# A hybrid transformer block in one core: the keys of 13 feed-forward blocks as seven products over both token halves, linear attention in buffers of its own, and a new order of the work

## The chip, the core and the metric

The kernel runs on one core of a Trainium2 chip. A core has five engines, each with an instruction queue that it works through in order: TensorE (PE, matmuls; its weight loads are listed apart as PEld), VectorE (DVE), ScalarE (ACT), GpSimd (POOL) and SyncE (SP, which here only issues DMAs). They wait for each other through semaphores. The metric is the device time of one execution in microseconds; the time before is 1154.61 us, the median of three runs (1153.1 to 1155.28).

## The reference

x has the shape (8, 512, 256): 8 batches of 512 tokens with 256 features, in float32. Four residual steps follow, each with a layer norm in front (LN):

```python
x = x + attn_a(LN(x))      # linear attention: l2norm(x Wq) * mean over tokens of l2norm(x Wk) * (x Wv)
x = x + ffn(LN(x))         # the first ffn, "f"
x = x + attn_b(LN(x))      # softmax attention, 16 heads of 64; the softmax runs over the queries
x = x + ffn(LN(x))         # the second ffn, "g", with the same weights
```

The ffn mixes each token with the one before it, with one weight per feature, and gates:

```python
xr = mu_r * x + (1 - mu_r) * x_prev
xk = mu_k * x + (1 - mu_k) * x_prev
out = sigmoid(xr @ Wr.T) * (square(relu(xk @ Wk.T)) @ Wv.T)
```

## The kernel before, in words

A batch is held as four tiles of 128 tokens, and most steps run on one half of a batch (256 tokens, h = 0 or 1). Features are put on the partitions by transposing, so a half is two chunks of 128 features by 256 tokens. All matmuls are in float32.

**Softmax attention** is the frame of the program. The 16 heads of a batch are 8 pairs; g counts pairs over all batches (64). For a pair, `scores` (L1007) makes four chunks of scores with small 64x64 matmuls (L1019), VectorE takes their maximum (nm, L1024), `exps` (L1029) makes the exponents e and their sums on ScalarE (L1035), `scale_v` (L1043) has VectorE invert the sums (rs, L1048) and GpSimd scale the values (vs, L1052), and `context` (L1059) multiplies e with vs (cx, L1072). `attend` (L1085) runs two pairs, with the scores of one beside the context of the other. The e tiles come from a pool of six buffers.

**Projections.** For batches after the first, queries, keys and values come from seven products in place of eight, in Strassen's manner: `seven` (L794) takes the two halves of the tokens and the two halves of the features as a 2x2 block matrix. Its weights' sums are made once (`sums_of_weights`, L745), the rows' sums once a batch with four GpSimd subtractions (`sums_of_rows`, L759, L775). Each chain of seven uses three PSUM banks; VectorE and ScalarE add the products up between the matmuls (L814, L824, L832, L866, L874), and three products (numbers 2, 3 and 4) are accumulated onto a bank that was read before.

**The ffn** (`ffn`, L523) runs half by half: mixing, the keys (L533, four matmuls of 128x256 for each half), relu and square on ScalarE (L540, L543), the gate r, the output o, and two element-wise steps (L552, L559). For batches 0 and 1, and for the last ffn g7, features get onto the partitions by PE transposes (`mixed_t`, L449). The other 13 ffns, f2 to f7 and g0 to g6, do it by DMA (`mixed_dma`, L487): GpSimd sets the 16-bit halves apart (L411), SP issues a DMA transpose (L416), GpSimd puts them together again (L420).

**Linear attention** (`linear`, L592; `queries`, L642; `mean`, L662; `front`, L678) shares the tiles xn, xp, xr and xk of the f ffns. There are two such sets: one for batch 1 and for g0 to g6 (True in tile names), one for all else (False). `add_front` (L570) begins linear attention of batch b when the whole first ffn of the batch ahead is done.

**The order** of all this is fixed when the program is built. Class `Order` (L77) is a planner: each piece of work is a generator that yields steps with an engine, an assumed duration and a time from which it can run; the planner keeps a clock for each engine and decides which step is issued next. Pieces have due times counted in pairs (`due_of`, L578). After each two pairs of heads, `until` (L212) issues what is due, and `fill` (L197) more, up to a share of the remaining PE work. `CHOICES` (L38) has a triple for each two pairs: an offset to that share, a slack for the other engines, and a number that shuffles the ranks. Each PSUM bank that a piece holds is tracked (`take`, `give`, `clear`).

**Loads and stores.** When both halves of g of batch b are done, SP stores them (L976) and loads x of batch b + 4, 512 KB (`load_x`, L266, its DMA on L271). SP's queue has these loads and stores and all DMA transposes. At the end, after the last context, the output projection y of batch 7 is followed by g7, with what is left of g6 between.

Of the kernel before, what the change touches and what calls it, by code (L numbers as in the profile page):

```python
# [9 lines left out]
U16 = mybir.dt.uint16  # L10
# [28 lines left out]
    (-4, 2, 90203), (-4, -1, 82533), (-6, 1, 13258), (1, 2, 55349), (6, -1, 0), (6, 0, 31648),  # L39
    (6, 1, 79266), (-6, 2, 0), (6, 2, 0), (-6, 0, 0), (6, 2, 32685), (0, 0, 0), (6, -1, 57850),  # L40
    (2, 2, 0), (-2, 0, 61030), (0, 0, 8722), (0, -1, 70803), (6, -1, 0), (1, 0, 423),
    (0, 0, 1350), (-1, 0, 93496), (-6, -1, 32755), (6, 1, 0), (1, 2, 25961), (4, 0, 78747),
    (1, 2, 30264), (0, 2, 52830), (4, 2, 36824), (6, 0, 37004), (4, -1, 19765), (-2, 1, 75445),
    (0, 0, 79050), (6, 1, 84670), (4, 1, 42587),
# [32 lines left out]
class Order:  # L77
# [40 lines left out]
    def clear(self, banks):  # L118

        for i in banks:  # L120
            while not unheld(self.banks[i]):
                c = self.banks[i]
                self.run(c if c.mark in self.marks else self.first(self.able()))
# [111 lines left out]
def kernel(ctx: ExitStack, tc: tile.TileContext, a: dict, out: bass.AP):  # L235
# [20 lines left out]
    epool = ctx.enter_context(tc.tile_pool(name="epool", bufs=6))  # L256
# [71 lines left out]
    def buffers(own):  # L328


        if own not in sets:
            s = {
                n: one.tile([P, 2, 512], F32, tag=f"{n}{own}", name=f"{n}{own}")
                for n in ("xr", "xk")
            }
            for n in ("xn", "xp"):
                s[n] = one.tile([P, 2, 2, HS + 1], F32, tag=f"{n}{own}", name=f"{n}{own}")
                nc.gpsimd.memset(s[n][:, 0, :, 0:1], 0.0)

            s["ka"], s["r"] = s["xn"], s["xk"]  # L340
            sets[own] = s
        return sets[own]

# [3 lines left out]

    def inner(t, h):
        return t[:, h, :, 1:]
# [5 lines left out]
    def normed(src, name, s, h, ready, early=False):  # L355
# [7 lines left out]
        xn, rstd = inner(s["xn"], h), small.tile([P, 2], F32, tag="rstd", name=f"rstd_{name}_{h}")  # L363
# [27 lines left out]
    def normed_t(src, name, s, h, ready, mark=None, early=False):  # L391

        ready = yield from normed(src, name, s, h, ready, early)
        xn = inner(s["xn"], h)
        ready = yield "T", 0.55, ready, -1, mark
        ps = bank(f"tr_{name}_{h}").rearrange("p (k s) -> p k s", k=KC)
        for kc in range(KC):
            for u in range(2):
                nc.tensor.transpose(
                    ps[:, kc, u * P : (u + 1) * P], xn[:, u, kc * P : (kc + 1) * P], ident  # L400
                )
        return ps, ready

    def normed_dma(src, name, s, h, ready, dst, mark=None):


        ready = yield from normed(src, name, s, h, ready)
        apart, turned = (s[n].bitcast(U16)[:, h, :] for n in ("xr", "xk"))
        ready = yield "G", 1.2, ready
        for u in range(2):  # L410
            nc.gpsimd.tensor_copy(  # L411
                apart.rearrange("p (l k u d) -> p l k u d", l=2, k=KC, u=2)[:, :, :, u, :],
                s["xn"].bitcast(U16)[:, h, u, 2:].rearrange("p (k d l) -> p l k d", l=2, k=KC),
            )
        ready = yield "S", 0.9, ready
        nc.sync.dma_start_transpose(  # L416
            out=turned.rearrange("p (g r) -> p g r", r=P), in_=apart
        )
        ready = yield "G", 1.25, ready, -1, mark
        nc.gpsimd.tensor_copy(  # L420
            dst().rearrange("p k (s l) -> p l k s", l=2),
            turned.rearrange("p (l k s) -> p l k s", l=2, k=KC),
        )
        return ready
# [23 lines left out]

    def mixed_t(xb, name, s, h, ready, xr, xk):  # L449
# [3 lines left out]

        parts = ((1, s["xn"]), (0, s["xp"]))
# [8 lines left out]
        for i, y in parts:  # L463
            for kc in range(KC):
                nc.scalar.activation(
                    y[:, h, kc, 1:], ps[:, kc, :], AF.Identity, scale=omu[:, i, kc : kc + 1]
                )
        order.marks[name, h] = ready
        if h == 1:
            ready = yield "V", 0.25, ready, -1, (name, 0)  # L470
            for i, y in parts:
                nc.vector.tensor_tensor(
                    y[:, 1, :, 0:1], edge[name], omu[:, i, :].unsqueeze(2), ALU.mult
                )
        for (i, y), dst in zip(parts, (xk, xr)):
            ready = yield "V", 0.79, ready
            for kc in range(KC):
                nc.vector.scalar_tensor_tensor(
                    dst[:, kc, :], ps[:, kc, :], mu[:, i, kc : kc + 1], y[:, h, kc, :HS],
# [7 lines left out]
    def mixed_dma(xb, name, s, h, ready, xr, xk):  # L487
# [4 lines left out]
            lambda: s["xr"].bitcast(U16)[:, h, :].rearrange("p (k s) -> p k s", k=KC),  # L492
# [6 lines left out]
        for i, dst in ((1, xk), (0, xr)):  # L499
# [7 lines left out]
            if h == 0:  # L507
                nc.vector.memset(ps[:, :, 0:1], 0.0)
            else:
                nc.vector.tensor_tensor(  # L510
                    ps[:, :, 0:1], edge[name], omu[:, i, :].unsqueeze(2), ALU.mult
                )
# [10 lines left out]
    def ffn(xb, name, s, h, ready, add_on, by_dma):  # L523
# [5 lines left out]
        done = yield "T", BANK, mixed  # L529
        ps = bank(f"k_{name}_{h}")  # L530
        for dc in range(KC):
            for kc in range(KC):
                nc.tensor.matmul(  # L533
                    ps[:, dc * HS : (dc + 1) * HS], lhsT=fk[:, kc, dc * P : (dc + 1) * P],
                    rhs=xk[:, kc, :], start=(kc == 0), stop=(kc == KC - 1),
                )
        done = yield "A", 0.6, done
        ka, r = inner(s["ka"], h), s["r"][:, h, :]
        ps = ps.rearrange("p (k s) -> p k s", k=KC)
        nc.scalar.activation(ka, ps, AF.Relu)  # L540
        order.give()
        squared = yield "A", 0.6, done
        nc.scalar.activation(ka, ka, AF.Square)  # L543
# [5 lines left out]
        ready = yield "T", BANK, squared  # L549
# [4 lines left out]
        return (yield from add_to(xb, h, r, ready, add_on))  # L554

# [14 lines left out]
    def add_front(b):  # L570


        if b in x and b not in begun and (b < 2 or (0 if b == 2 else b - 1) in fronts):
            begun.add(b)
            for h in range(2):
                order.add(linear(b, h), *due_of(b))
# [15 lines left out]
    def linear(b, h):  # L592

        xb, s = x[b], buffers(b == 1)
        ready = asked[b] + X_LANDS[min(b, 2)] + h / 2
        xt, kv = inner(s["xp"], h), inner(s["ka"], h)
# [5 lines left out]
        else:  # L602
            ready = yield from normed_dma(
                xb, f"a{b}", s, h, ready, lambda: s["xp"].bitcast(U16)[:, h, :, 2:]
# [4 lines left out]
        for u in range(2):  # L609
# [10 lines left out]
            sq = one.tile([P, D], F32, tag="sq", name=f"sqk_{b}_{h}_{u}")  # L620
            nc.scalar.activation(sq, ps[:, :D], AF.Square, accum_out=ss[:, u : u + 1])
# [20 lines left out]
    def queries(b, h):  # L642

        s = buffers(b == 1)
        xt = inner(s["xp"], h)
# [4 lines left out]
        for u in range(2):  # L650
            sq = one.tile([P, D], F32, tag="sq", name=f"sqq_{b}_{h}_{u}")
            nc.scalar.activation(
                sq, ps[:, u * D : (u + 1) * D], AF.Square, accum_out=ss[:, u : u + 1]
# [24 lines left out]
    def front(b, h, gf, ready):  # L678
# [4 lines left out]
        rn, qs = halves[b, h], tiles(s["r"], h)  # L683
# [4 lines left out]
        ready = yield from add_to(xb, h, s["r"][:, h, :], ready, adder(b))  # L688
        ready = yield from ffn(xb, f"f{b}", s, h, ready, adder(b), b >= 2)
# [23 lines left out]
        else:  # L713
            if b:
                order.add(sums_of_rows(b, ready), NP * b - 1, NP)
            fronts.add(b)
            if b:
                add_front(b + 1)
# [13 lines left out]
    }  # L732

# [11 lines left out]
    def sums_of_weights(w, tag, split, after):  # L745
# [3 lines left out]
        (a11, a21), (a12, a22) = v  # L749
        s1, s2, s4 = (s[:, i, :].rearrange("p (g c) -> p g c", g=a11.shape[1]) for i in range(3))  # L750
        for dst, x0, x1, op in (
            (s1, a21, a22, ALU.add), (s2, s1, a11, ALU.subtract), (s4, a12, s2, ALU.subtract),
            (a21, a11, a21, ALU.subtract),
        ):
            ready = yield "G", 1.3, 0.0, -1, after
# [29 lines left out]
    def blocks_of_weights(w, sums, split, g):  # L785
# [5 lines left out]
        s1, s2, s4 = (sums[:, i, g * n : (g + 1) * n] for i in range(3))  # L791
        return [a11, a12, s4, a22, s1, s2, s3]

    def seven(name, sums, mul, c, begin, join):  # L794
# [5 lines left out]
        (c11, c12), (c21, c22) = c  # L800

        def product(n):
            ready = yield "T", FAST, 0.0, -1, sums
# [4 lines left out]
            return i, ps, ps.rearrange("p (u s) -> p u s", u=2), ready  # L808
# [4 lines left out]
        u2 = yield "V", 0.62, max(ready, u1)  # L813
# [4 lines left out]
        p2 = yield "T", FAST, u1, -1, None, False  # L818
        mul(b1, 2, False)
        yield from begin(ps1, c11, max(p2, u2))  # L820
        order.give(i1)
        i5, b5, ps5, p5 = yield from product(5)
        c22_done = yield "V", 0.62, max(p5, u3)
        nc.vector.tensor_tensor(c22, ps5, c22, ALU.add)  # L824
        p4 = yield "T", FAST, u3, -1, None, False
        mul(b7, 4, False)
        yield from join(ps7, c21, c12, p4, False)
        order.give(i7)
        p3 = yield "T", FAST, c22_done, -1, None, False
        mul(b5, 3, False)  # L830
        order.marks[name] = yield "V", 0.62, p3
        nc.vector.tensor_tensor(c12, ps5, c12, ALU.add)  # L832
        order.give(i5)

# [110 lines left out]
    def project_out(b, half):  # L945
# [3 lines left out]
        for tp in range(NT // 2):  # L949
# [10 lines left out]
            if half == 1:  # L960
                order.add(tail(b, tp, ready), NP * (b + 2) + 1, lead)
# [3 lines left out]
    def tail(b, h, ready):  # L965
# [7 lines left out]
        order.marks["g", b, h] = yield from ffn(x[b], f"g{b}", buffers(not last), h, ready, add_on, not last)  # L973
# [156 lines left out]
    order.add(sums_of_weights(av, "sums_v", split_values, "plain_v"), 5)  # L1130
    order.until(-1)
# [5 lines left out]
    total += 2 * FAST  # L1137
# [76 lines left out]
```

## Time and profile before

| | us |
|---|---|
| median of three runs | 1154.61 |
| the profiled execution | 1151.33 |
| its span, first to last instruction | 1149.6 |
| PE busy | 1127.1 |
| VectorE (DVE) busy | 780.2 |
| ScalarE (ACT) busy | 671.8 |
| GpSimd (POOL) busy | 440.3 |

The clock granted to TensorE is full throughout. How to read the lines: a group of instructions has the source line, the engine, the operation, the tiles (out<-in), the shape and the count, then its busy time in us and the mean of one in ns, then the idle time of the engine just before these instructions, and what ended it. A line of the timeline has the start and the duration in us, and in brackets the idle time of the engine before it. PE matmuls overlap in the pipeline, so a mean of 379 ns stands for less time on the path. Names are those of the program; xkFalse is the tile xk of the set False.

### The profile page before, as it was taken

What the parts mean: (1) busy time and instruction counts of PE and PEld (TensorE: products, weight loads), DVE (VectorE), ACT (ScalarE), POOL (GpSimd) and SP (SyncE); (2) the same over time, 40 slices, a digit from 0 to 9 for tenths busy, and PEclk for the clock granted to TensorE, in tenths of its full rate; (3) what the DMA queues carried; (4) which work ended last, traced back from release to release, by engine and by line L of the source; (5) the groups of instructions that cost most, each with busy time, mean ns of one, the idle gap of its engine ahead of it and who ended that gap; (6) DMA issues with size and microseconds to landing.
All of it is one profiled execution on the core that took longest, in us unless ns stands there. A gap on an engine that the chain in (4) does not pass through costs nothing.

```text
span 1149.6 us, 19062 instructions
## 1 busy us (share of the span) xinstructions
PE 1127.1 (98%) x7020; PEld 702.6 (61%) x7020; DVE 780.2 (68%) x1403; ACT 671.8 (58%) x1763; POOL 440.3 (38%) x708
## 2 busy tenths in 40 slices
PE   7999999999999999999999899999999999999998
PEld 4645565856556676666667466567665666566557
DVE  5767658676667775867667576667676676666663
ACT  3547646475565654666544675565665367644753
POOL 4455224334324464335612436243453534312201
PEclk9999999999999999999999999999999999999999
DMA  8000001100101101011100201001010011000001
GB/s 297 1 1 2 1 1 19 20 10 11 28 1 42 24 19 28 1 46 29 37 1 1 54 12 38 11 17 40 10 29 19 19 19 25 5 10 19 11 1 37
DMA packets 61180, 28.63 MB, mean 25 GB/s; under 512 B 51456, under 2 KB 59648, under 8 KB 60576
## 3 DMA queue, kind: packets, MB, share of 16 engines
q1 hardware_dynamic: 59936, 25.70, 9.0%
q8 instruction: 56, 0.92, 0.3%
q10 hardware_dynamic: 864, 1.05, 0.3%
q0 software_dynamic: 288, 0.67, 0.2%
q14 instruction: 36, 0.29, 0.1%
HBM read 10.63 MB, written 4.19 MB: 13 GB/s over the span
## 4 chain that ended last, share of the span: by engine, by line
PE 75%; DVE 1%; DMA 0%; issue 0%; ACT 0%; POOL 0%; POOLq 0%; DVEq 0%
PE cx L1072 16%; PE sc L1019 15%; PE m_qk L858 13%; PE y L432 8%; PE m_v L894 6%; PE kv L613 3%; PE o_g L432 2%; PE r_g L432 2%; PE k_g L533 2%; PE k_f L533 2%; PE r_f L432 2%; PE o_f L432 2%; PE q L432 2%; DVE nm L1024 1%; DMA xkFalse<-xrFalse 0%
## 5 line engine op out<-in xcount | busy, mean ns | idle before, releaser
L1035 ACT ACTIVATE e<-sc,nm 128x512 f32<-128x512 f32 x512 | 347.1, 690 | 119.8 <-DVE nm L1024 119.8
L1024 DVE TENSOR_REDUCE nm<-sc 128x2 f32<-128x1024 f32 x256 | 308.9, 1218 | 76.6 <-PE sc L1019 75.7
L1072 PE MATMUL cx<-e,vs 64*64 64x512 f32 x2048 | 265.2, 590 | 5.1 <-POOL vs L1052 4.0
L1019 PE MATMUL sc<-qk 64*64 64x512 f32 x2048 | 266.8, 593 | 1.0 <-DVE qk L832 0.9
L1052 POOL TENSOR_TENSOR vs<-v,rs 128x256 f32<-128x256 f32 x128 | 78.5, 614 | 356.7 <-DVE rs L1048 348.6
L1072 PEld LDWEIGHTS cx<-e,vs 64*64 64x64 f32 x2048 | 84.3, 133 | 143.3 <-issue 117.8
L1019 PEld LDWEIGHTS sc<-qk 64*64 64x64 f32 x2048 | 75.0, 132 | 136.8 <-issue 90.7
L432 PE MATMUL y<-al,ctx 128*128 128x256 f32 x512 | 116.2, 380 | 0.0
L432 PEld LDWEIGHTS y<-al,ctx 128*128 128x128 f32 x512 | 97.0, 190 | 15.8 <-ACT e L1035 1.6
L1035 ACT ACTIVATION_READ_ACCUMULATOR e<-sc,nm 128x1 f32 x512 | 105.2, 205 | 0.0
L866 ACT ACTIVATE qk<-m_qk,bias 128x256 f32<-128x256 f32 x124 | 52.2, 476 | 56.9 <-PE m_qk L858 53.5
L1080 DVE TENSOR_TENSOR ctx<-cx,ctx 128x512 f32<-128x512 f32 x64 | 44.3, 692 | 47.6 <-ACT ctx L1079 47.6
L874 DVE SCALAR_TENSOR_TENSOR qk<-m_qk,dbias,qk 128x256 f32<-128x256 f32 x124 | 54.0, 477 | 18.3 <-PE m_qk L858 17.3
L958 DVE TENSOR_TENSOR x<-y,x 128x512 f32<-128x512 f32 x32 | 22.1, 690 | 55.3 <-PE y L432 55.3
L613 PE MATMUL kv<-wkv,xpFalse 128*128 128x512 f32 x112 | 52.2, 599 | 0.0
L1079 ACT COPY ctx<-cx 128x512 f32<-128x512 f32 x64 | 37.4, 585 | 13.8 <-PE cx L1072 13.8
L619 ACT COPY av<-kv 128x256 f32<-128x256 f32 x32 | 11.9, 373 | 54.8 <-PE kv L613 52.2
L411 POOL COPY xrFalse<-xnFalse 128x512 uint16<-128x512 uint16 x68 | 39.6, 616 | 8.5 <-ACT xnFalse L385 8.5
L559 POOL TENSOR_TENSOR x<-x,xkFalse 128x512 f32<-128x512 f32 x24 | 31.2, 1303 | 27.2 <-issue 8.7
L858 PE MATMUL m_qk<-xta,aq 128*128 128x256 f32 x124 | 39.1, 397 | 0.0
L858 PE MATMUL m_qk<-xta,sums_q 128*128 128x256 f32 x124 | 38.1, 389 | 0.7 <-DVE qk L814 0.7
L858 PE MATMUL m_qk<-xts,aq 128*128 128x256 f32 x124 | 37.2, 382 | 0.3 <-DVE qk L874 0.3
(243 smaller groups left out, 1881.6 us busy)
## 6 DMA issues: line engine op xcount, KB each, us to landing
out<-x SPq DMA_DIRECT2D x16, 256.0 KB, 2.1
x<-in_x SPq DMA_DIRECT2D x6, 512.0 KB, 4.3
aq<-in_aq SPq DMA_DIRECT2D x1, 1024.0 KB, 6.2
ak<-in_ak SPq DMA_DIRECT2D x1, 1024.0 KB, 8.1
av<-in_av SPq DMA_DIRECT2D x1, 1024.0 KB, 10.2
al<-in_al SPq DMA_DIRECT2D x1, 1024.0 KB, 12.2
xkFalse<-xrFalse SPq DMA_TRANSPOSE x34, 3.1
x<-in_x ACTq DMA_DIRECT2D x4, 128.0 KB, 4.0
```

Of the source, the lines that this page charges most:

```text
L432: nc.tensor.matmul(ps[:, u * D : (u + 1) * D], lhsT=lhs[i][:, u * P : (u + 1) * P], rhs=rhs[i], start=(i == 0), stop=(i == n - 1),)
L533: nc.tensor.matmul(ps[:, dc * HS : (dc + 1) * HS], lhsT=fk[:, kc, dc * P : (dc + 1) * P], rhs=xk[:, kc, :], start=(kc == 0), stop=(kc == K ...
L613: nc.tensor.matmul(ps, lhsT=xt[:, kc, u * P : (u + 1) * P], rhs=wkv[:, kc, :], start=(kc == 0), stop=(kc == KC - 1),)
L858: nc.tensor.matmul(ps[:, w * HS : (w + 1) * HS], lhsT=lhs[w][n - 1], rhs=block_of_rows(b, n), start=start and w == 0, stop=True, skip_grou ...
L866: nc.scalar.activation(dst[:, w, :], ps[:, w, :], AF.Identity, bias=bias[:, w, p : p + 1])
L874: nc.vector.scalar_tensor_tensor(dst[:, w, :], ps[:, w, :], dbias[:, w, p // 2 : p // 2 + 1], part[:, w, :], ALU.add, ALU.add,)
L894: nc.tensor.matmul(ps[:, u * HS : (u + 1) * HS], lhsT=block_of_rows(b, n)[:, u * P : (u + 1) * P], rhs=rhs[n - 1], start=start and u == 0, ...
L1019: nc.tensor.matmul(ps[m * HD : (m + 1) * HD, j, :], lhsT=kt[hs, keys], rhs=qt[hs, :], start=True, stop=True,)
L1024: nc.vector.tensor_reduce(nm, ps, AX.X, ALU.max, negate=True)
L1035: nc.scalar.activation(e[:, j, :], ps[:, j, :], AF.Exp, bias=nm[:, j : j + 1], accum_out=sums[g, h][:, c % 2, j : j + 1],)
L1052: nc.gpsimd.tensor_tensor(vs, vh[b, p // 4][:, 2 * h : 2 * h + 2, cols].rearrange("p t (j d) -> p t j d", j=2), rs.unsqueeze(3).to_broadca ...
L1072: nc.tensor.matmul(cx[m][j * HD : (j + 1) * HD, :], lhsT=vsc[g, c // 2][ks, c % 2, j, :], rhs=es[g, c][ks, j, :], start=(c == 0), stop=(c ...
```

## The change

1. **Keys in seven products.** For the 13 ffns with DMA transposes the keys of both halves are made together, when both are mixed, by a new function `keys`. It makes four GpSimd subtractions of 128x256, runs `seven` at half size (one matmul of 128x256 for each product, one PSUM bank each), and then relu and square of each half from SBUF. The sums of the weights fk are made once (four subtractions of 128x128).
2. **Linear attention in its own buffers** for batches from 2 on (`buffers_linear`); it begins when linear attention of the batch ahead is done, and so runs beside that batch's first ffn. An ffn of batch b waits for the one of batch b - 1.
3. **Buffers.** xp goes, xn has no extra column any more, `mixed_t` and the mixing write the previous token's part straight into the target tile; squares whose values nobody needs go to tiles that are free at the time. There are five e buffers in place of six.
4. **Order.** `clear` prefers steps that take no bank; PE's planned total is lower by 13 half products; `CHOICES` has new numbers.

```diff
-    (-4, 2, 90203), (-4, -1, 82533), (-6, 1, 13258), (1, 2, 55349), (6, -1, 0), (6, 0, 31648),
...
+    (-4, 2, 90203), (0, 0, 43155), (0, 2, 0), (-2, 2, 77416), (1, 0, 8249), (-2, 1, 93964),
...
-    epool = ctx.enter_context(tc.tile_pool(name="epool", bufs=6))
+    epool = ctx.enter_context(tc.tile_pool(name="epool", bufs=5))
...
+    def buffers_linear(b):
+        if b < 2:
+            return buffers(b == 1)
+        if "linear" not in sets:
+            n = {n: one.tile([P, 2, 512], F32, tag=f"{n}l", name=f"{n}l") for n in ("xn", "xr")}
+            sets["linear"] = {"xn": n["xn"], "xk": n["xn"], "ka": n["xn"], "xr": n["xr"], "r": n["xr"]}
+        return sets["linear"]
...
+        if by_dma:
+            r, mark = s["xr"][:, h, :], (name, "k", h)
+            if both((name, "k")):
+                order.add(keys(name, s, mixed), *due)
+        else:
...
+    def keys(name, s, ready):
+        xk = [chunks(s["xk"], h) for h in range(2)]
+        (b11, b12), (b21, b22) = ([xk[h][:, kc, :] for h in range(2)] for kc in range(KC))
+        t = s["sums"]
...
+        for dst, x0, x1 in (
+            (t[:, 1, :], b22, b12), (b12, b12, b11), (t[:, 0, :], b22, b12),
+            (t[:, 2, :], b21, t[:, 0, :]),
+        ):
+            ready = yield "G", 0.8, ready
+            nc.gpsimd.tensor_tensor(dst, x0, x1, ALU.subtract)
...
+        def mul(ps, n, start):
+            nc.tensor.matmul(
+                ps[:, :HS], lhsT=lhs[n - 1], rhs=rhs[n - 1], start=start, stop=True,
+                skip_group_check=True,
+            )
+        def begin(ps, dst, ready):
+            ready = yield "A", 0.36, ready
+            nc.scalar.copy(dst, ps)
+            return ready
+        def join(ps, dst, part, ready, first):
+            ready = yield "V", 0.36, ready
+            nc.vector.tensor_tensor(dst, ps, part, ALU.add)
+            return ready
+        def through(h, ready):
+            for f in (AF.Relu, AF.Square):
+                ready = yield "A", 0.6, ready
+                nc.scalar.activation(ka[h], ka[h], f)
+            order.marks[name, "k", h] = ready
+        c = [[ka[h][:, dc, :] for h in range(2)] for dc in range(KC)]
+        yield from seven(f"k_{name}", (name, "t"), mul, c, begin, join, 0.5, through)
...
-        if b in x and b not in begun and (b < 2 or (0 if b == 2 else b - 1) in fronts):
+        if b in x and b not in begun and (b < 3 or b - 1 in fronts):
...
-        ready = yield from add_to(xb, h, s["r"][:, h, :], ready, adder(b))
-        ready = yield from ffn(xb, f"f{b}", s, h, ready, adder(b), b >= 2)
+        ready = yield from add_to(xb, h, q[:, h, :], ready, adder(b))
+        if b > 1:
+            if both(f"l{b}"):
+                fronts.add(b)
+                add_front(b + 1)
+            ready = yield "V", 0.0, ready, -1, (f"n{0 if b == 2 else b - 1}", h)
+        ready = yield from ffn(xb, f"f{b}", s, h, ready, adder(b), b >= 2, due_of(b))
...
-    total += 2 * FAST
+    total += 2 * FAST - 13 * FAST / 2
```

## The prediction

> **What bounds the kernel now.** I read the page first: engine shares, then the costliest groups.
>
> ```profile
> PE 1127.1 (98%) x7020; PEld 702.6 (61%) x7020; DVE 780.2 (68%) x1403; ACT 671.8 (58%) x1763; POOL 440.3 (38%) x708
> L1072 PE MATMUL cx<-e,vs 64*64 64x512 f32 x2048 | 265.2, 590 | 5.1 <-POOL vs L1052 4.0
> L858 PE MATMUL m_qk<-xta,aq 128*128 128x256 f32 x124 | 39.1, 397 | 0.0
> L858 PE MATMUL m_qk<-xta,sums_q 128*128 128x256 f32 x124 | 38.1, 389 | 0.7 <-DVE qk L814 0.7
> L858 PE MATMUL m_qk<-xts,aq 128*128 128x256 f32 x124 | 37.2, 382 | 0.3 <-DVE qk L874 0.3
> L858 PE MATMUL m_qk<-xta,ak 128*128 128x256 f32 x124 | 36.9, 379 | 0.0
> ```
>
> TensorE (PE) is busy for 98% of the span, the next engine (VectorE) for 68%. A busy PE is not a PE at its peak, so I looked at the chain that ended last for a stretch with nothing to wait for:
>
> ```profile
> 269.10 3.45 PE y L432 x16
> ```
>
> An fp32 matmul leaves two records, so 16 records are 8 matmuls of 128x256: 3.45 / 8 = 0.431 us each. At that rate (0.86 us for 512 columns and for a group of four 64x64 ones) the PE work adds up to about 1100 us of the 1149.6 us span. The rest, near 49 us, is 6.9 us before the first matmul, 4.6 after the last, about 10 in the first 100 us, and small losses at each change of work. So time comes from fewer PE cycles, or from the few long PE waits. Two of these are the 4.0 us that cx (L1072) waits for POOL. The timeline around the longer one:
>
> ```profile
> 639.27 0.38 SPq L271 DMA_DIRECT2D x<-in_x  x1
> 639.75 1.25 SPq L416 DMA_TRANSPOSE xkFalse<-xrFalse  x1
> 644.62 1.33 POOL L420 COPY xrFalse<-xkFalse 128x1024 uint16<-128x1024 uint16 x1 [5.38 <-DMA xkFalse<-xrFalse]
> 645.88 1.19 POOL L1052 TENSOR_TENSOR vs<-v,rs 128x256 f32<-128x256 f32 x2
> 646.55 1.09 PE L1072 MATMUL cx<-e,vs 64*64 64x512 f32 x8 [3.39 <-POOL vs L1052]
> ```
>
> A transpose is issued half a microsecond behind the 512 KB load of the next x. It lands after 4.8 us, where the median is 3.1. POOL runs in order, so the copy out of the transpose holds the scaled values (vs), and PE waits 3.39 us. The same happens at 773 us (load 773.23, transpose 773.77, cx idle 0.65): together the 4.0 us of the row.
>
> **The change, part by part.** Sums are made against the profiled execution, 1151.33 us (its span and 1.7 us around it); the median of the runs is 3.28 us above it, and I carry that over.
>
> (a) Seven products. 13 ffns make the keys with 8 matmuls of 128x256 for both halves now (L533), and with 7 afterwards. The built program has 3531 matmuls against 3544 before: -13. Gain 13 x 0.431 = 5.6 us, all on the path.
>
> (b) What the seven products need. Nearest rows, same sizes:
>
> ```profile
> L775 POOL TENSOR_TENSOR xts<-xta 128x256 f32<-128x256 f32 x16 | 11.7, 733 | 1.5 <-PE m_qk L858 1.0
> L625 DVE TENSOR_TENSOR xnFalse<-kv,av 128x256 f32<-128x256 f32 x28 | 11.8, 421 | 25.6 <-ACT sqk L621 25.6
> L619 ACT COPY av<-kv 128x256 f32<-128x256 f32 x32 | 11.9, 373 | 54.8 <-PE kv L613 52.2 <-DVE xnTrue L625 2.0
> ```
>
> Per ffn: four subtractions on POOL, 4 x 0.733 = 2.9 us; five adds on DVE, 5 x 0.421 = 2.1; two copies on ACT, 0.75; relu and square stay. Over 13: POOL +38 us (440 to 478, 42% of the span), DVE +27 (70%), ACT +10 (59%). None becomes the bound; what counts is whether PE waits inside a chain. A product that accumulates onto a bank must wait until the bank was read. The pairs' chains show the price: m_qk groups that follow such a read take 39.1, 38.1 and 37.2 us where the undisturbed ones take 36.9, so 3.7 us over 31 chains, 0.12 each; 13 x 0.12 = 1.6 us. Bounds: 0.4 by the idle column (1.0 us over 31), and 4.6 at 0.35 a chain. The chain of g0 is the tight one in the new order: its last five products stand together, the two on one bank 0.86 us apart, where 0.59 (matmul) + 0.42 (add) + about 0.1 of handing over = 1.1 are needed. I take +1.6, as it is the row of the same structure.
>
> Here the Trainium skill speaks against the change (SBUF — State Buffer, Who interferes with whom): GpSimd and VectorE share a port pair under an exclusive lock; a VectorE instruction with two SBUF inputs and a GpSimd one that reads SBUF block each other for a whole instruction. The row that bears on it:
>
> ```profile
> L685 DVE SCALAR_TENSOR_TENSOR xkFalse<-xkFalse,rnq,gf x28: 451/478/1498, 23.0 to 905.3; 128x256 f32<-128x256 f32 x28
> 903.09 3.69 DVE L685 SCALAR_TENSOR_TENSOR xkFalse<-xkFalse,rnq,gf 128x256 f32<-128x256 f32 x4
> ```
>
> Four of these should take 1.9 us; beside POOL's adds they took 3.69, and the m_qk chain behind them on DVE stalled. Carried over to all 65 new DVE adds at the group's excess (mean 741 on the page's by-shape rows against 478), the cost would be 65 x 0.26 = 17 us of DVE. By the rule it is nearly nothing: the new adds have one input in PSUM, so the 38 us of POOL (3% of the span) can meet only the 66 VectorE instructions that read two SBUF tiles (L685, L636, L559). I take the rule's 0, and keep 2 us for the range.
>
> (c) The order around the loads. In the new program the transpose next to each load of x stands 20, 20, 18 and 26 us of PE work behind it (before: 16, 1, 1 and 1). Linear attention of the loaded batch must normalise first, and no other ffn half stands there. No copy out of a transpose is closer than 7.1 us of PE work to the cx that needs the vs behind it (before: 4.7, at the 3.39 us wait). So both waits go: -4.0. What is late next there is cx's own input, which PE finds ready everywhere else. Queues: SP has the same 84 instructions; POOL gets the 52 subtractions in front of vs. The worst place is at 153 us of PE work, where 14 us of POOL work (statistics of f2 and a3, four xts, two copies) stand in the 14 us ahead of a cx: nearest row, the 1.04 us that PE loses at 160 us now. Same size, taken as 0, bounds -1 and +3.
>
> (d) The tail. The ffn g7 runs alone at the end:
>
> ```profile
> 1128.40 1.89 PE L432 MATMUL r_g<-fr,xrTrue 128*128 128x256 f32 x8
> 1132.30 1.12 ACT L385 ACTIVATE xnFalse<-x,shift_g,rstd_g 128x256 f32<-128x256 f32 x2
> 1134.02 0.60 PE L399 MATMUL tr_g<-ident,xnFalse 128*128 128x128 f32 x4
> ```
>
> The last y ends at 1128.40; normalising takes until 1133.42, 5.0 us; PE fills them with r_g, a transpose and both o_g: 1.72 + 0.44 + 3.45 = 5.6. In the new order r_g went earlier; the cover is one product, o_g, transpose, o_g: 0.43 + 1.72 + 0.44 + 1.72 = 4.3. The ACT queue must also pass the edge and four activations of the first half (0.15 + 0.86 + 0.86, from 2.8 us on) ahead of the 1.12: 5.8. Between 1.1 and 1.6 us are uncovered: +1.5.
>
> (e) At nothing: five e buffers in place of six. A cx frees its buffer 1.93 us after the scores beside it start (0.86 + 1.07); their exponent is ready to run at 2.36, so it hides by 0.43 us; if that cover is gone, ACT's slack at the end of the pair takes it; up to 2. The separate buffers and the shuffled order: between -4 (the crowded place at 906 to 917, 3.1 us, and the one at 160 don't come back) and +4 (two such places arise elsewhere); taken as 0, since the number of such places is that of an order, and both are made by the same planner. The startup has the same PE order up to the first projected pair.
>
> Sum: -5.6 + 1.6 - 4.0 + 1.5 = -6.5. Profiled execution 1144.8; median 1148.1.
>
> **The rivals.** (1) A clean order: the waits in chains (1.6) and tail (1.5) are hidden, and the 906 and 160 us places go (4.1): -5.6 - 4.0 - 4.1 = -13.7, 1140.9. For it: linear attention has buffers of its own, so its front need not press into one stretch with values and pairs, as at 903. Against: DVE has 65 more instructions to place. (2) No change within 0.2%: the gain of 9.6 is eaten by chains at their upper bound (4.6), the tail (1.6) and one new place of 3 us: -0.4, 1154.2. (3) Slower: POOL in order. The four subtractions of a key set, 2.9 us, stand ahead of vs, and cx waits as at 646 us, 3.4 us each time. The gain without it is 6.5, so it decides from the second of 13 sets on; at four of them 13.6 - 6.5 = +7.1, 1161.7. Against: in the listing only three sets (at 442, 552 and 948 us of PE work) stand close ahead of a vs, and at 547 us of PE work in the present order 5.2 us of POOL work ahead of a vs cost PE nothing. That the change doesn't do what it says is excluded by the count of matmuls.
>
> **How the numbers follow.** The forecast has 0.60 (1144 to 1152), rival 1 0.23, rival 2 0.09, rival 3 0.08. About 0.2% is what a measurement can tell here, 2.3 us: faster means under 1152.3. That gives 0.84 faster (the forecast's uppermost edge and rival 1 both lie there; 0.01 more from rival 2's lower edge), 0.08 same, 0.08 slower. The range leaves out rival 3, half of rival 2 and the far end of rival 1: 1141 to 1153.5.
>
> **What would show it.** (a) 13 matmuls fewer, 0.43 us each; span 5.6 shorter if all else stays. (b) The waits of k groups for DVE: near 1.6 us in sum, busy means above 0.379 where they accumulate. (c) cx waiting for vs under 1 us in sum, transposes landing at 3.1 us. (d) An idle PE of 1 to 1.6 us ahead of the last tr_g. (e) L685's successor slower than 478 ns only beside POOL. I would be wrong if cx waits for vs at several sets of keys, or if PE's small losses per 50 us (0.8 now) grow throughout.

## The result and the profile after

The changed kernel takes 1147.26 us (median of 4 runs, 1146.73 to 1147.59), the kernel before, in 4 runs, 1154.65 (1153.1 to 1155.28): a ratio of 0.9938, 95% interval 0.992 to 0.9955, so 7.4 us less. The forecast was 1148.1. The profiled execution takes 1146.73 us with a span of 1144.8; before it was 1151.33 and 1149.6. The spans differ by only 4.8, and that needs a word: the profiled execution of before was a fast one, 3.3 us under its median, while that of after is 0.5 under its own. Of the 53 runs of the kernel before that were made beside the experiments, five are like it (1151.03 to 1151.64, with a mean granted clock of 1.0); the other 48 took 1152.97 to 1156.98 at mean clocks of 0.996 to 0.999. All ten runs of the changed kernel have 1.0.

The page of the changed kernel, engine shares and the groups that answer to those of before (columns: busy us, mean ns of one, idle before):

```profile
PE 1125.2 (98%) x6994; PEld 699.2 (61%) x6994; DVE 806.0 (70%) x1474; ACT 679.5 (59%) x1789; POOL 478.9 (42%) x760
L1095 PE MATMUL sc<-qk 64*64 64x512 f32 x2048 | 270.1, 594 | 2.6 <-DVE qk L903 1.7
L1148 PE MATMUL cx<-e,vs 64*64 64x512 f32 x2048 | 269.1, 589 | 0.0
L931 PE MATMUL m_qk<-xta,sums_q 128*128 128x256 f32 x124 | 38.0, 388 | 1.0 <-DVE qk L893 0.9
```

26 records, 13 matmuls, are gone. The engines' shares are as forecast to within 2 us (807, 681 and 478 were the sums). The 4.0 us of cx waiting for vs is gone; the scores (sc) wait 2.6 us where it was 1.0. Four of the waits of TensorE in the changed kernel (us in total, times, longest):

```profile
PE sc L1095 <- DVE qk L903: 1.7, 4, 0.4
PE sc L1095 <- ACT xnl L392: 0.9, 1, 0.9
PE tr_g L406 <- ACT xnFalse L392: 0.5, 2, 0.4
PE m_k_g L591 <- DVE xnTrue L893: 0.3, 1, 0.3
```

The new key products (m_k) wait 0.3 us for DVE to have read their bank. A wait that the trace can attribute is only part of what is lost. So I also measured the loss itself: for each group of like matmul records, the time from its first record to the next group's first record, less the records at full rate (0.431 us for a 128x256 matmul, the chain's own rate; 0.86 for a four-tile group of 512 columns). The sums, by what comes next, from my own reading of the traces; the kernels b_load and a_noside are explained below:

| loss of PE, us | before | b_load | after | a_noside |
|---|---|---|---|---|
| first 100 us | 10.0 | 9.9 | 10.1 | 9.4 |
| ahead of cx | 8.2 | 4.0 | 2.2 | 2.1 |
| ahead of sc | 5.8 | 5.7 | 8.8 | 8.2 |
| ahead of m_qk | 9.7 | 9.7 | 10.1 | 9.8 |
| ahead of m_k or k (keys) | 0.5 | 0.5 | 1.1 | 0.4 |
| ahead of y and r | 0.4 | 0.4 | 2.2 | 1.4 |
| all else but the tail | 1.9 | 1.8 | 1.9 | 1.9 |
| tail (from 12 us ahead of the last cx) | 0.8 | 0.8 | 2.2 | 2.2 |
| sum | 37.2 | 32.7 | 38.6 | 35.4 |
| span | 1149.6 | 1144.5 | 1144.8 | 1142.2 |

The losses did not shrink. PE's work fell by 5.6 us, the losses rose by 1.4, and the first matmul came 0.5 earlier: 4.7 of the 4.8 us. Yet cx lost 6.0 less: the rest grew by 7.4 us. The experiments ask what the fall in cx is worth in most executions, and what the growth comes from.

### The profile page after: what moved, and what is told of

The parts are those of the page before. It is cut to its first block, busy times and chain, and to the rows that moved or that the text cites. A ratio compares the mean times of both kernels' runs of the same rounds, so it can differ in the third digit from the quotient of the medians.

```text
span 1144.8 us, 19233 instructions
## 1 busy us (share of the span) xinstructions
PE 1125.2 (98%) x6994; PEld 699.2 (61%) x6994; DVE 806.0 (70%) x1474; ACT 679.5 (59%) x1789; POOL 478.9 (42%) x760
## 5 line engine op out<-in xcount | busy, mean ns | idle before, releaser
L1095 PE MATMUL sc<-qk 64*64 64x512 f32 x2048 | 270.1, 594 | 2.6 <-DVE qk L903 1.7
L1148 PE MATMUL cx<-e,vs 64*64 64x512 f32 x2048 | 269.1, 589 | 0.0
L1148 PEld LDWEIGHTS cx<-e,vs 64*64 64x64 f32 x2048 | 87.2, 133 | 136.9 <-issue 114.5
L1031 DVE TENSOR_TENSOR x<-y,x 128x512 f32<-128x512 f32 x32 | 22.0, 687 | 35.5 <-PE y L440 35.4
L672 PE MATMUL kv<-wkv,xrl 128*128 128x512 f32 x96 | 44.9, 595 | 0.0
L931 PE MATMUL m_qk<-xta,ak 128*128 128x256 f32 x124 | 36.9, 379 | 0.0
L931 PE MATMUL m_qk<-xts,ak 128*128 128x256 f32 x124 | 36.9, 379 | 0.0
L931 PE MATMUL m_qk<-xta,sums_k 128*128 128x256 f32 x124 | 36.9, 379 | 0.0
## 6 DMA issues: line engine op xcount, KB each, us to landing
ak<-in_ak SPq DMA_DIRECT2D x1, 1024.0 KB, 10.1
```

The lines of the kernel that those rows point to most:

```text
L672: nc.tensor.matmul(ps, lhsT=xt[:, kc, u * P : (u + 1) * P], rhs=wkv[:, kc, :], start=(kc == 0), stop=(kc == KC - 1),)
L931: nc.tensor.matmul(ps[:, w * HS : (w + 1) * HS], lhsT=lhs[w][n - 1], rhs=block_of_rows(b, n), start=start and w == 0, stop=True, skip_grou ...
L1095: nc.tensor.matmul(ps[m * HD : (m + 1) * HD, j, :], lhsT=kt[hs, keys], rhs=qt[hs, :], start=True, stop=True,)
L1148: nc.tensor.matmul(cx[m][j * HD : (j + 1) * HD, :], lhsT=vsc[g, c // 2][ks, c % 2, j, :], rhs=es[g, c][ks, j, :], start=(c == 0), stop=(c ...
```

## The experiments

My theory was the forecast's sum. The rivals were that the loads are worth little outside one profile, that the key chains (bank waits, or the queues of DVE and POOL behind them) cost much more than 1.6 us, and that the order table does the work. Each kernel was run 5 to 18 times; the medians of the kernel before beside them, in the three sets of runs, were 1154.05, 1154.12 and 1154.0. Where two kernels of different sets are compared, it is by what each stands under the kernel before beside it.

**The changed kernel again, as the yardstick.** No edit.

> The changed kernel once more, unaltered, beside the other runs of this series. Theory (13 matmuls, 5.6 us, and the two waits of cx behind the loads, 4.0 us, less 3 us of new waits): 6 to 7.5 us below the kernel before, ratio 0.9935 to 0.995. Rival (the profiled executions alone are right, 1146.7 against 1151.3): 4.6 us, ratio 0.996.

1147.09 us (1146.25 to 1147.48), ratio 0.9938 (0.9925 to 0.9952): 7.0 us less, within the theory's range and clear of the rival. The 19 runs of before spread over 5.8 us, these over 1.2.

**The load alone.** The kernel before; the next x is loaded on the same queue, but behind the next transpose:

```diff
-            nc.sync.dma_start(out=x[b], in_=rows)
+            if b < 4:
+                nc.sync.dma_start(out=x[b], in_=rows)
+            else:
+                held_load.append((x[b], rows))
...
         nc.sync.dma_start_transpose(
...
+        while held_load:
+            t, rows_in = held_load.pop()
+            nc.sync.dma_start(out=t, in_=rows_in)
```

> The kernel before with one thing moved: SP issues the load of each x from batch 4 on behind the next DMA transpose, not ahead of it. All other queues keep their order. Theory (the wait of cx for vs at 646 and 780 us comes from the transpose landing late behind the load): both waits go, -4 us (-3 to -5.5), and the runs scatter less. Rival (POOL is late there anyway, and the transpose only the last of what it waits for): under 1 us.

1147.71 us (1146.31 to 1148.25), ratio 0.9944 (0.9929 to 0.9959): 6.3 us, more than my range of 3 to 5.5 and nearly all that the whole change brings, with no product fewer. The timeline of this kernel at the place that the prediction showed (start, duration, engine, what; idle before in brackets):

```profile
636.46 0.37 SPq L982 DMA_DIRECT2D out<-x  x1
636.93 1.28 SPq L419 DMA_TRANSPOSE xkFalse<-xrFalse  x1
638.89 0.38 SPq L424 DMA_DIRECT2D x<-in_x  x1
640.16 1.34 POOL L426 COPY xrFalse<-xkFalse 128x1024 uint16<-128x1024 uint16 x1 [1.54 <-DMA xkFalse<-xrFalse]
641.43 0.61 POOL L1058 TENSOR_TENSOR vs<-v,rs 128x256 f32<-128x256 f32 x1
642.36 1.07 PE L1078 MATMUL cx<-e,vs 64*64 64x512 f32 x8
```

The transpose goes first and is copied out from 3.2 us after its issue on; cx starts at 642.36 with no idle time. In the table only the row of cx moves (8.2 to 4.0). The runs of this kernel spread over 1.9 us.

Comparing this with the timeline of before shows a part of the wait that the prediction did not see. In both, SP issues the store of an x (out<-x) ahead of load and transpose. In before the load waits on SP until that store has landed, and the transpose waits behind it, though its input is ready (POOL's copy to it ends at 635.80). First the store in before, then the row of the four loads in SP's waits there:

```profile
637.06 0.38 SPq L976 DMA_DIRECT2D out<-x  x1
SPq L271 <- DMA out<-x: 7.0, 4, 1.8
```

From the store's issue to the transpose's it takes 2.7 us in before (637.06 to 639.75) and 0.5 here. So of the 3.9 us by which the copy out comes earlier here, counted from the store, 2.2 are this place in the queue and 1.6 the faster landing.

**Five e buffers alone.** The kernel before, `bufs=6` to `bufs=5` in the pool of e.

> The kernel before with five e buffers in place of six; every queue keeps its order. Theory (a cx frees its buffer 0.4 us before the next exponent can run): 0 to +1 us. Rival (the sixth buffer lets ScalarE run ahead while PE waits, so its loss lengthens every wait): +2 us or more.

1154.76 us in 14 runs, ratio 1.0004 (0.9996 to 1.0013): nothing, as forecast. Its profile, of an execution of 1156.46 us, is worth more than its time, since the same collision is in it:

```profile
640.38 0.38 SPq L271 DMA_DIRECT2D x<-in_x  x1
640.86 1.25 SPq L416 DMA_TRANSPOSE xkFalse<-xrFalse  x1
647.40 1.32 POOL L420 COPY xrFalse<-xkFalse 128x1024 uint16<-128x1024 uint16 x1 [7.06 <-DMA xkFalse<-xrFalse]
649.32 1.98 PE L1072 MATMUL cx<-e,vs 64*64 64x512 f32 x8 [5.04 <-POOL vs L1052]
```

The same two issues, 0.48 us apart; the transpose is ready for the copy only after 6.5 us (4.8 in the profile of before), and PE waits 5.04 us where it was 3.39. Nor is the wait all of it. Behind it TensorE ran at half its clock; the first line has a stretch, its length, the busy time and count of PE, PEld, DVE, ACT and POOL in it, then the granted clock (0.50), DMA share and GB/s; the second is the group of scores behind the cx above:

```profile
649.30:653.80 4.50, 4.48 (x24) 1.45 (x28) 0.72 (x1) 1.45 (x4) 0.54 (x1) 0.50 0.00 0
651.08 1.93 PE L1019 MATMUL sc<-qk 64*64 64x512 f32 x8
```

Three groups, which start 0.86 us apart at full clock, here take 1.76, 1.71 and 1.41 us: 2.3 us more. In the profile of before the clock stayed at 1.00 after the wait of 3.39 us. Together with 1.7 us of longer waits for vs and 1.0 in the first 100 us, where neither plays a part, this is nearly all of the difference between the two spans (5.1 us). The half-clock stretch lasts 6.8 us, which takes 0.3% off the mean clock of a span; 30 of the 53 runs of before have a mean of 0.996 or 0.997, as this one has 0.996. So, as an estimate from these figures, more than half of the executions of before paid for such a stretch too. That the longer wait brings it on is read from these two traces and was not tried. The collision's price changes from one execution to the next, and the profile of before had a cheap one.

**The eighth product back.** The changed kernel, with product 1 made twice in each of the 13 chains:

```diff
-            nc.tensor.matmul(
+            for _ in range(2 if n == 1 else 1):
+              nc.tensor.matmul(
```

> The changed kernel with one matmul of 128x256 too many in each of the 13 key chains (product 1 is made twice, the second over the first), so that PE has the number of matmuls of the kernel before; queues and order stay else. Theory (PE is the bound at these places): 13 x 0.43 = +5.6 us against the changed kernel, 1152.7. Rival (PE waits in these chains anyway, and the matmul fills the wait): +2 us or less.

1152.73 us in 18 runs, ratio 0.9984 (0.9977 to 0.9991): 5.6 above the changed kernel. A product fewer is worth its full 0.43 us in place.

**The banks.** The changed kernel; three of the seven products go to the other half of their bank instead of onto it, which was meant to spare them the wait for a read:

```diff
-                ps[:, :HS], lhsT=lhs[n - 1], rhs=rhs[n - 1], start=start, stop=True,
-                skip_group_check=True,
+                ps[:, :HS] if start else ps[:, HS:], lhsT=lhs[n - 1], rhs=rhs[n - 1],
+                start=True, stop=True, skip_group_check=True,
```

> The changed kernel with the waits of the keys' second products taken away: products 2, 4 and 3 of the 13 key chains are written to the free half of the bank and not accumulated, so that they need not wait for VectorE or ScalarE to have read the bank, and what follows reads that half. The sums of the keys are left out by this; all instructions, sizes and queue orders stay. Theory (the chains' own waits are 1.1 us in the trace, the rest of what the keys cost lies in VectorE's queue): -0.5 to -1.5 us against the changed kernel. Rival (waits on the bank are the cost of 13 chains, hidden in lengthened matmuls): -3 us or more.

1146.73 us (1146.34 to 1146.98), ratio 0.9935 (0.9922 to 0.9949): 0.4 less than the changed kernel. But the edit did not do what it was meant to. The loss ahead of m_k is 1.1 us here, as in the changed kernel, and the wait that the list there named is here too, at the same product:

```profile
PE m_k_g L591 <- DVE xnTrue L895: 0.3, 1, 0.3
```

Product 3 still waits until the add L895 has read the other half of the bank. The runs overlap those of the changed kernel, so the 0.4 us are no price of anything, and neither theory nor rival was tested. What the bank waits can cost is bounded by the trace alone: 1.1 us are lost ahead of all key products.

**The side work away.** Three kernels: the changed one without the five DVE adds of each chain (a_nodve), without the four POOL subtractions, with the products reading tiles that are there (a_nopool), and without both (a_noside). The edits of the last, in `keys` and in `seven` (the other two sums of `seven` go the same way):

```diff
-            nc.gpsimd.tensor_tensor(dst, x0, x1, ALU.subtract)
...
-        rhs = [b11, b21, b22, t[:, 2, :], b12, t[:, 0, :], t[:, 1, :]]
+        rhs = [b11, b21, b22, b21, b12, b22, b12]
...
-            nc.vector.tensor_tensor(dst, ps, part, ALU.add)
...
-        nc.vector.tensor_tensor(c12, ps6, c11, ALU.add)
+        if not through:
+            nc.vector.tensor_tensor(c12, ps6, c11, ALU.add)
```

> The same with only the five VectorE adds of each key chain left out (the keys' sums are not formed), the subtractions stay. Theory (VectorE's queue carries most of it, as scores, y and the second products wait for VectorE or for ScalarE behind it): -2 to -4 us against the changed kernel. Rival (GpSimd carries it): under 1 us.

> The same with only the four GpSimd subtractions of each key chain left out (the products read the mixed rows as they are), the adds stay. Theory (GpSimd has slack in this order; twice the work cost 3.9 us since no time was planned for it): 0 to -1 us against the changed kernel. Rival (GpSimd's queue is as tight as it looked when the work was doubled): -3 us or more.

> The changed kernel without the side work of the 13 key chains: the four GpSimd subtractions and the five VectorE adds of each are left out (so the keys are not the sums they should be, the products read the mixed rows as they are); 91 products, two copies, relu and square stay, and the order of all else. Theory (the two proven parts, 5.6 us of products and 6.4 us of loads, would give 12 us, and the 5 us that are missing from the measured 7 are waits for this side work and for what is queued behind it): -3 to -5 us against the changed kernel. Rival (they are the order's own waits, wherever they stand): under 1 us.

Without the adds 1145.6 us (ratio 0.9931, 0.9918 to 0.9943), 1.4 less than the changed kernel and under my range; without the subtractions 1145.7 (0.9928, 0.9916 to 0.9941), 1.3 less, between the theories; without both 1144.18 (0.9918, 0.9906 to 0.9931), 2.9 less, just short of my range. The two nearly add up. Without the adds no key product has to wait for one, so bank waits for DVE are part of the 1.4. Two of the waits of TensorE in the last:

```profile
PE sc L1096 <- DVE qk L904: 1.7, 4, 0.4
PE sc L1096 <- ACT xnl L392: 0.9, 1, 0.9
```

The wait of the key products is gone from the list, but the scores still wait 1.7 us for the pairs' last add. The 2.9 us are scattered: between the two profiled executions of the table, whose spans differ by 2.6, they are keys 0.7, y and r 0.8, sc 0.6 and m_qk 0.3. (The 0.7 of the first 100 us is not the side work, since the first key chain begins at 245.6 us, and the first matmul came 0.6 later in a_noside.) The scores' waits belong to the order, which places them right behind a key set's last product. Here one of the four, in the changed kernel:

```profile
385.77 0.59 PE L591 MATMUL m_k_f<-xkFalse,sums_f 128*128 128x256 f32 x2
...
385.97 0.69 DVE L903 TENSOR_TENSOR qk<-m_qk,qk 128x512 f32<-128x512 f32 x1
...
386.81 1.09 PE L1095 MATMUL sc<-qk 64*64 64x512 f32 x8 [0.45 <-DVE qk L903]
```

One product covers the pair's add only in part. No key add delays it: the one ahead of it on DVE ends at 385.88, before the pair's last product does.

**The side work doubled.** The changed kernel with each subtraction twice (a_pool2, 38 us more of POOL), or three of the five adds twice (a_dve2, 16 us of adds more on DVE), planned at no time:

```diff
+            if dst is b12:
+                nc.gpsimd.tensor_tensor(t[:, 0, :], b22, b21, ALU.subtract)
+            else:
+                nc.gpsimd.tensor_tensor(dst, x0, x1, ALU.subtract)
             nc.gpsimd.tensor_tensor(dst, x0, x1, ALU.subtract)
```

```diff
-            nc.vector.tensor_tensor(dst, ps, part, ALU.add)
+            for _ in range(2):
+                nc.vector.tensor_tensor(dst, ps, part, ALU.add)
...
-        nc.vector.tensor_tensor(c12, ps6, c11, ALU.add)
+        for _ in range(2 if through else 1):
+            nc.vector.tensor_tensor(c12, ps6, c11, ALU.add)
```

> The changed kernel with each of the four GpSimd subtractions of a key set made twice (the second time over the first, or into a tile that is written again): 52 more of 0.73 us, 38 us of GpSimd, planned at no time; order stays. Theory (GpSimd has slack, and few sets stand close ahead of a vs): 0 to +3 us against the changed kernel. Rival (what the products save is lost in GpSimd's queue): doubling costs as much as is lost, +5 us or more.

> The changed kernel with three of the five VectorE adds of a key set made twice with the same result: 39 more of 0.42 us, 16 us of VectorE, planned at no time; order stays. Theory (part of what the products save is lost because scores, products and o wait for VectorE behind these adds): +3 to +7 us against the changed kernel. Rival (VectorE has slack there too): under +1.5 us.

1151.05 us (ratio 0.9973, 0.9961 to 0.9984) and 1150.6 (0.9965, 0.9952 to 0.9977): 3.9 and 3.4 more than the changed kernel. POOL lies between the two theories, DVE at the low end of what I expected. With POOL doubled, a line is back in the list of waits:

```profile
PE cx L1152 <- POOL vs L1132: 2.5, 3, 1.2
```

The loss ahead of cx grows from 2.2 to 5.8 us, which is nearly the whole cost. This is the third rival's mechanism, and it begins only with the subtractions doubled: three places, the longest 1.2 us. With DVE doubled the losses ahead of m_qk, sc and the keys grow by 1.1, 1.0 and 0.8.

**The order table.** The kernel before with its table all zeros (b_plain), and the changed kernel with the table of before (a_oldorder):

```diff
+CHOICES = ((0, 0, 0),) * 34
```

> The kernel before with all numbers of its order table zero: no offsets, no shuffling. One of its four late loads has a transpose within 1 us of PE work behind it, as three have in the kernel before. Theory (the load's place is worth more than the table): within 3 us of the kernel before, if that one collision doesn't meet a waiting cx below it. Rival (the table is worth a lot): +5 us or more.

> The changed kernel with the order table of the kernel before (the changed program gives the same numbers another meaning). Theory (a table fits one program alone; all zeros cost the kernel before 70 us): +30 to +90 us against the changed kernel. Rival (the table's numbers carry over in part, or the new structure needs them less): under +15 us.

1224.22 us (ratio 1.0601, 1.0586 to 1.0615) and 1208.19 (1.0477, 1.0461 to 1.0494). The first was far outside my expectation of 3 us: the table is worth 70 us to its program. The second lies within its expectation: the table of before costs the changed program 61 us against its own. (That program with all zeros was not run.) The granted clock was 0.986 and 0.987 in these two, where the other profiled executions have 0.996 to 1.0: each trace has seven stretches of half clock ahead of its end, 34 and 31 us together, which can have cost 17 and 15 us at most. In the trace of the second, cx, which waited 1.0 us for DVE in the profile of before, waits for whatever DVE was given ahead of its inputs (four of the longest rows):

```profile
PE cx L1148 <- DVE xnl L683: 7.8, 3, 5.3
PE cx L1148 <- DVE xkTrue L523: 4.9, 2, 2.5
PE m_qk L931 <- DVE qk L893: 4.1, 2, 3.5
PE sc L1095 <- DVE qk L903: 4.1, 5, 1.0
```

So the new order can't be taken off the changed kernel to price the rest: each program was timed with a table of its own or badly.

## Why the prediction was right, and where its terms were not

The median was 0.8 us off, with two of its terms too small in opposite directions. The profiled execution was forecast at 1144.8 and took 1146.73, so the step from there to the median, 3.28 us, was off as well: it measured 0.5.

(a) Seven products, -5.6: shown. 13 matmuls fewer, and +5.6 when they are put back.

(b) "A product that accumulates onto a bank must wait until the bank was read", +1.6: the sign is right, size and place are not. The trace names 0.3 us of such waits, and ahead of all key products only 0.7 us go when the side work goes. The cost is 2.9 us, and it is that of the side work: 1.4 by DVE's and 1.3 by POOL's, each alone. I had looked for its price inside the key chain; the trace shows most of it elsewhere, ahead of y, r, sc and m_qk. That it gets there through the engines' queues is argued from this and from the doubling; the waits were not traced one by one, and the bank waits alone have no price, since a_free kept them. The 0.12 us a chain carried over from the pairs was no price for that.

The lock of the Trainium skill (SBUF — State Buffer, Who interferes with whom) was taken at nothing for the new adds, since one of their inputs lies in PSUM. The trace agrees: the DVE adds of the key chains took 415 to 420 ns in the mean, and none of the 65 took more than 426, though 31 ran beside POOL for over 0.1 us. The instruction with two SBUF inputs, at L744 now, still pays:

```profile
L744 DVE SCALAR_TENSOR_TENSOR xrl<-xrl,rnq,gf 128x256 f32<-128x256 f32 x24 | 15.3, 689 | 2.9 <-ACT gf L731 2.9
L744 DVE SCALAR_TENSOR_TENSOR xkFalse<-xkFalse,rnq,gf 128x256 f32<-128x256 f32 x4 | 1.7, 473 | 3.2 <-ACT gf L731 3.2
```

At 689 against 473 ns those 24 lose 5.2 us of DVE. It lies in seven of them, of 637 to 1489 ns, and each of these overlaps a POOL instruction of 128x256 or more (on x, v, vs or sums); the other 17 took 455 to 485. So it happens only beside POOL, as forecast. At the excess of these rows the new adds would have taken 14 us more of DVE; they took what the forecast counted.

(c) The transposes behind the loads, -4.0: the collision is right, the mechanism was seen in part, and the size is wrong. In the changed kernel the transpose behind the load that stands at 645 us is issued 17 us later:

```profile
645.47 0.38 SPq L273 DMA_DIRECT2D x<-in_x  x1
...
662.71 1.24 SPq L424 DMA_TRANSPOSE xnl<-xrl  x1
```

No wait of cx for vs is in the list. But the step took the waits of one execution (3.39 + 0.65) for the price; moving the load alone brings 6.3 at the median. The slow landing, which I read, is 1.6 us of the delay; the 2.2 us that the transpose stood on SP behind the load's own wait I missed. And a longer wait came with half a clock behind it: in the profile of b_e5 the two waits and the clock make 5.7 + 2.3 = 8.0 us, in that of before 4.0, and the median lies between. I carried the 3.28 us between profiled execution and median over as a constant, though most of it was this term: it went away with the collision, and after's profile stands 0.5 under its median.

(d) The tail, +1.5: the trace shows +1.4 (0.8 to 2.2). The timeline of TensorE in the changed kernel:

```profile
1126.49 1.99 PE L440 MATMUL o_g<-fv,xnTrue 128*128 128x256 f32 x8
1128.85 0.33 PE L406 MATMUL tr_g<-ident,xnFalse 128*128 128x128 f32 x1 [0.37 <-ACT xnFalse L392]
1129.34 0.55 PE L406 MATMUL tr_g<-ident,xnFalse 128*128 128x128 f32 x3 [0.16 <-ACT xnFalse L392]
```

The idle columns show 0.5 of it, since ends of matmuls are modelled; from the first o_g record to the first tr_g record there are 2.36 us, where eight records take 1.72. With 0.44 more among the four tr_g, 1.1 us are the cover running out, as forecast; the other 0.3 are the balance of small losses ahead of that, among them 0.66 at a key product at 1116.0 us. No kernel with the old tail was run.

(e) The buffers of e, 0: shown. The order, 0: the trace has +2.5 ahead of sc and -1.9 ahead of cx that neither the load nor the side work explains (a_noside against b_load); they nearly cancel.

The sum by what was measured: -5.6 - 6.3 + 2.9 + 1.4 = -7.6, against -7.4 and, beside the experiments, -7.0. Between 0.2 and 0.6 us are left for the rest of the order, if the load's 6.3 us, measured on the kernel before, hold for the changed one. The terms of opposite sign were 2.3 and 1.3 us too small, which is why the sum came out well. That they cancelled so far is luck; the range covered it.

Of the rivals, the clean order fell: the waits and the tail are there (the losses ahead of cx did fall by 1.9 us more than the load explains; I did not trace them to its places at 906 and 160 us). No change fell with the time. The slower one didn't come, but its mechanism is real: with the subtractions doubled, cx begins to wait for vs. Open is why no transpose stands behind a load in the new order. Linear attention's own buffers and the new table came together, and were not timed apart: the old table on the new program collapses for other reasons.

## What to carry to other kernels

A wait in one profiled execution is a sample: where its length rests on a transfer, look at how far the runs of the kernel scatter before pricing its removal, and expect the scatter to go with it. Look at the granted clock behind the wait too, and at what each entry ahead of it in the issuing queue was itself waiting for. Price new side work by the queues that it enters, not only by the chain that it serves: engines at 42% and 70% passed 2.9 us of it on to the bound one. And before crediting a rewrite, try the cheapest part alone: here a few lines that move a load were worth nearly as much as the whole.

## What was not expected of the hardware

A DMA transpose issued half a microsecond behind a 512 KB load on the same queue landed after 4.8 us in one execution and 6.4 in another, where the median is 3.1. Without such a pair the changed kernel and its variants under the new table spread over 0.6 to 1.9 us, b_load over 1.9; with it the kernel before spread over 3.5 to 5.8 in the three sets.

After a wait of 5.04 us TensorE was granted half its clock for 6.8 us; after one of 3.39 us it kept the full clock.

Work on engines that are far from full is not free when each runs in order: 38 us more of POOL, at 42% busy, cost 3.9 us, about a tenth; 16 us more of adds on DVE, at 70%, cost 3.4, about a fifth.
